# Depthwise taps as row stacks on quarters of TensorE's columns, and five PSUM banks in one pool

## The chip, the cores and the metric

The kernel runs on one core of one Trainium2 chip. The metric is the device time of one execution in microseconds. Of the kernel before, three runs gave 18203.6, 18205.7 and 18205.72 us; the median is 18205.7 us.

Names of the engines: PE is TensorE (PEld its weight loads), DVE is VectorE, ACT is ScalarE, POOL is GpSimd, and SP is the queue that issues every DMA of this kernel.

## What is computed

Two residual layers on 8 images of 56 x 56 pixels and 192 channels, all in float32. The first is a group normalisation and attention with depthwise 3x3 convolutions for queries (stride 1) and for keys and values (stride 2). The second is a state-space scan in four directions; the change touches its input, the depthwise 3x3 convolution over 384 channels, and the PSUM banks in which its scan works:

```
xz = einsum('bhwc,oc->bhwo', gn(x), in_proj_w)
xa, z = split(xz, 2)
xc = silu(depthwise_conv3x3(xa, conv_w, 'SAME') + conv_b)      # 384 channels
xs = [xc by rows, xc by columns, both reversed]                # 4 directions, 3136 steps
dts, Bs, Cs = split(x_proj_weight @ xs)                        # 12, 16 and 16 rows
delta = softplus(dt_projs @ dts + bias)
h = exp(delta * A) * h + delta * B * xs                        # 16 states a channel
y = sum over the states of h * C, + D * xs
out = x + out_proj(layernorm(y summed over the directions) * silu(z))
```

## The kernel before

**Tiling.** The 3136 pixels of an image are 7 chunks (`NCH`) of T = 448 pixels, which is 8 rows (`RPC`) of 56. The 384 channels of the second layer are NJ = 3 blocks of 128 partitions; the 192 outer channels are 2 blocks of 96.

**The scan** takes the 8 images ("batches") one after the other, each in four directions of 7 chunks with 16 states: 448 steps a batch. A step is done by these generators, each with its own line:

- `row_loads`: a DMA spreads one row of B over 128 partitions (`bb`, five buffers); for some states a row of C too (`cb`).
- `inputs_made` (L1119): POOL multiplies it with delta * x into a state tile `h` (seven buffers), 3 x 448 elements wide.
- `decays` (L1133): ACT makes three exponentials `da`, one for each channel block, each into one PSUM bank.
- `scans` (L1150): DVE runs three scans over `h` with `da`; the bank is free after its scan.
- `turned` (L1196): PE transposes `h` by quarters of 112 pixels into a PSUM bank `ht`; `scaled` (L1212): ACT copies it into `g` and multiplies with C on the way; `back` (L1230): PE transposes `g` back and adds it up in the three banks `y`. For 3 or 4 of the 16 states POOL does this instead (`by_pool`, L1248 and L1252), and `summed` (L1267) adds the result into `y`.
- `evicted` (L1282, L1284): DVE adds `y` into `yacc`.

**The front** prepares the next batch while the scan of one runs: normalisation, first-layer convolutions (L615 and L452), attention (L756, L765), then the second layer's projection `project` (L853), its depthwise convolution (L452 again), and `x_proj` (L936 to L953), which makes the rows and the steps. Batch 0's front runs alone ahead of the first scan, with eight PSUM banks to itself. `finish` (L984 to L1033) ends a batch. Batch 7 has no front beside it.

**The convolution in question.** `project` takes the channel blocks j in turn. For each chunk it makes a projection in a PSUM bank, and `xa_out` (L818) has DVE write it with its bias into `xa`, one tile of 128 x 56 x 56. Then, for each chunk, nine matmuls (`TAPS`, `conv_rows`, L452) multiply a shifted view of `xa` with a 128 x 128 diagonal matrix of one tap's weights, all adding up in one bank; at an image's border the view is cut. The diagonals come from DRAM (`dgx_d`, 576 KB a block). `xv_out` (L824) has ACT copy the bank into `xv`, one tile for a block, and `stored` applies Silu (L830) and writes both pixel orders to DRAM (`xch`, `xcw`). The next block's projections need the one `xa` free, and its convolution the one `xv`.

**What sets the order.** Every engine runs its instructions in an order that is fixed when the program is built. A small planner (`Sched`) simulates the engines: each generator yields (engine, cost, what it reads, what it writes), and the planner gives the instruction that can start first, less a rank that favours some generators. DMAs carry a landing time with a margin of 3 us. A `Ring` hands out buffers in turn; a `Share` hands out the free tile of a common set whose last use is oldest, up to a limit `most`. The front is held to a pace (`pace`): its planned PE time may run 12 us ahead of or behind a share of the batch, 87% of it over the first three directions. Where the planner sees PE idle for more than 0.45 us, it puts filler matmuls of 64 columns (`warm`, L1363).

**PSUM during the scan**: three banks for `y`; two for the exponentials, a ring (`pa`, `rda`); and three (`pb`, `three`) shared by `ht`, two at most, and by all of front and finish (`bank1`), one at most.

## Time and profile before

| | |
|---|---|
| median of three runs | 18205.7 us |
| profiled execution | 18215.8 us, of which the span of the program is 18214.1 us |
| first scan starts (end of batch 0's front and first steps) | 814 us |
| batches 0 to 7, from first scan to the next batch's | 2273, 2231, 2212, 2205, 2208, 2206, 2212, 1799 us |
| busy: PE, DVE, ACT, POOL | 16706, 14152, 14224, 15561 us |
| moved by DMA | 2159 MB, 119 GB/s; engines 39.7% busy on the main queue |
| granted PE clock, mean | 0.982 |

A line of a group reads: source line, engine, operation, output <- inputs, their shapes, count | busy time in us, mean ns of one | idle time of the engine just before them, and what released it. A line of the waits reads: who waited <- for what: us in total, times, longest. A line of the timeline reads: start, length, engine, line, operation, operands, count, and in brackets idle time before it with its releaser. Busy time of PE counts each matmul record to its modelled end, so records that follow closely overlap. A stretch's busy time counts work of all lines in it.

### The profile page before, as it was taken

To read this page: it belongs to the slowest core of one execution; us is meant where nothing else is said; L and a number is where in the kernel's file an instruction comes from. 1 tells how busy PE (TensorE), PEld (TensorE's weight loads), DVE (VectorE), ACT (ScalarE), POOL (GpSimd) and SP (SyncE) were. 2 spreads that over 40 slices of the span, in tenths; PEclk is the share of its full clock that TensorE was granted. 3 is DMA by queue.
4 is the path that set the end of the run, shared out by engine and by line. 5 is a ranking of instruction groups with operands and counts; after the bars stand their busy time and mean duration, and the time that the engine had idled before them with its cause. 6 is when DMAs were issued, how large, how long until landed. Compare 5 with 4: busy or idle time off the path is not lost. (4 is left out here: it accounts for less than half of the span.)

```text
span 18214.1 us, 279960 instructions
## 1 busy us (share of the span) xinstructions
PE 16706.4 (92%) x99872; PEld 11743.7 (64%) x99872; DVE 14151.5 (78%) x17811; ACT 14223.5 (78%) x25030; POOL 15560.9 (85%) x5200
## 2 busy tenths in 40 slices
PE   8799999999999999999999999999999999999998
PEld 4466666666666666666666666666666666667776
DVE  2277777788878788787887877878878788888998
ACT  2377788687877878778787887878888787888888
POOL 0288899888998889888898889988899888999998
PEclk9899999999999999999999999999999999999999
DMA  1353345433453334533344334553345433453332
GB/s 54 115 161 90 94 142 158 119 90 107 140 170 97 94 112 139 163 99 95 116 147 152 99 92 120 150 150 95 96 127 155 135 93 95 135 153 120 97 96 78
DMA packets 1363539, 2158.99 MB, mean 119 GB/s; under 512 B 176112, under 2 KB 1346016, under 8 KB 1359072
## 3 DMA queue, kind: packets, MB, share of 16 engines
q1 hardware_dynamic: 1362144, 2141.09, 39.7%
q8 instruction: 791, 12.96, 0.3%
q14 instruction: 604, 4.95, 0.1%
HBM read 1649.41 MB, written 491.21 MB: 118 GB/s over the span
## 5 line engine op out<-in xcount | busy, mean ns | idle before, releaser
L1150 DVE TENSOR_TENSOR_SCAN h<-da,newc,h 128x448 f32<-128x448 f32 x9216 | 10104.9, 1137 | 1970.7 <-ACT da L1133 1380.5
L1119 POOL TENSOR_TENSOR h<-du_s,bb 128x1344 f32<-128x1344 f32 x3584 | 10825.3, 3053 | 927.5 <-PE ht L1196 816.2
L1133 ACT ACTIVATE da<-dl_s,acoef 128x448 f32<-128x448 f32 x10752 | 6750.8, 638 | 1756.9 <-DVE h L1150 1705.7
L1212 ACT ACTIVATE g<-ht,ct_s 112x384 f32<-112x384 f32 x10864 | 5847.5, 575 | 936.1 <-PE ht L1196 771.3
L1230 PEld LDWEIGHTS y<-ident,g 112*128 112x128 f32 x32592 | 3564.4, 142 | 2902.0 <-ACT g L1212 1954.4
L1230 PE MATMUL y<-ident,g 112*128 112x112 f32 x32592 | 4799.3, 268 | 654.3 <-ACT g L1212 530.1
L1196 PE MATMUL ht<-ident,h 128*112 128x128 f32 x32592 | 4944.2, 276 | 122.5 <-ACT g L1212 46.6
L1196 PEld LDWEIGHTS ht<-ident,h 128*112 128x112 f32 x32592 | 3683.2, 135 | 482.7 <-DVE h L1150 147.3
L1150 DVE TENSOR_TENSOR_SCAN h<-da,h 128x448 f32<-128x448 f32 x1536 | 1607.5, 1078 | 459.6 <-ACT da L1133 410.9
L1248 POOL TENSOR_TENSOR yp<-h,cb 128x1344 f32<-128x1344 f32 x448 | 1366.3, 3050 | 407.6 <-PE y L1267 173.7
L1248 POOL TENSOR_TENSOR h<-h,cb 128x1344 f32<-128x1344 f32 x420 | 1281.6, 3051 | 292.0 <-issue 171.9
L1363 PE MATMUL y<-zeros 128*128 128x64 f32 x11648 | 1486.5, 271 | 0.0
L1363 PEld LDWEIGHTS y<-zeros 128*128 128x128 f32 x11648 | 1444.5, 194 | 50.2 <-issue 50.2
L920 POOL TENSOR_TENSOR v<-v,xs 128x1344 f32<-128x1344 f32 x224 | 677.3, 3043 | 824.7 <-DMA dl<-v 773.6
L1252 POOL TENSOR_TENSOR yp<-yp,h 128x1344 f32<-128x1344 f32 x420 | 1280.1, 3048 | 32.2
L452 PE MATMUL bank<-xa,dg 128*128 128x440 f32 (+2 forms) x3024 | 1237.1, 535 | 24.2 <-ACT xv L824 19.2
L1267 PE MATMUL y<-yp,ident 128*128 128x448 f32 x2688 | 1223.4, 546 | 10.7 <-POOL yp L1252 10.2
L756 PE MATMUL bank<-qT,kT 128*112 128x448 f32 x2352 | 1074.5, 573 | 138.6 <-DVE oT L719 82.9
L765 PE MATMUL bank<-pT,vt 112*128 112x448 f32 x2352 | 999.9, 543 | 12.4 <-ACT g L1212 6.6
L706 ACT ACTIVATE pT<-bank,nsh 112x448 f32<-112x448 f32 x1176 | 740.1, 632 | 207.2 <-PE bank L756 167.1
L452 PE MATMUL bank<-band,dgq 96*96 96x440 f32 (+3 forms) x2016 | 806.4, 532 | 10.7 <-ACT hq L582 7.7
L452 PEld LDWEIGHTS bank<-xa,dg 128*128 128x128 f32 x3024 | 525.8, 191 | 364.6 <-issue 289.9
(146 smaller groups left out, 11082.0 us busy)
## 6 DMA issues: line engine op xcount, KB each, us to landing
bb<-rows SPq DMA_DIRECT2D x3584, 224.0 KB, 3.4
cb<-rows SPq DMA_DIRECT2D x868, 224.0 KB, 3.7
dl<-v SPq DMA_DIRECT2D x224, 672.0 KB, 5.0
du<-v SPq DMA_DIRECT2D x224, 672.0 KB, 6.1
du_s<-du SPq DMA_DIRECT2D x224, 672.0 KB, 4.5
dl_s<-dl SPq DMA_DIRECT2D x224, 672.0 KB, 4.6
xt<-x1d SPq DMA_DIRECT2D x224, 336.0 KB, 4.6
xch<-xv SPq DMA_DIRECT2D x24, 1568.0 KB, 7.3
```

Source lines behind the costliest of these rows:

```text
L452: nc.tensor.matmul(out[:, o0:o1, a:b], lhs, img(lo, hi)[:, :, a + dx - 1:b + dx - 1], start=(t == TAPS[0]), stop=(t == TAPS[-1]))
L756: nc.tensor.matmul(ps.ap[:TP, :T], kts[h][:, kb * TP:(kb + 1) * TP], qh.ap, start=True, stop=True)
L1119: nc.gpsimd.tensor_tensor(h.ap, du.ap, bb.ap.unsqueeze(1).to_broadcast([128, NJ, T]), ALU.mult)
L1133: nc.scalar.activation(da.ap[:, :T], dl.ap[:, j], AF.Exp, scale=acoef[:, k * NJ + j, n:n + 1])
L1150: nc.vector.tensor_tensor_scan(h.ap[:, j, rev], da.ap[:, 0:T][:, rev], h.ap[:, j, rev], news[i - 1].ap[:, j, n:n + 1] if ci else 0.0, ALU. ...
L1196: nc.tensor.transpose(ht.ap[:TP, j * 128:(j + 1) * 128], h.ap[:, j, s * TP:(s + 1) * TP], ident)
L1212: nc.scalar.activation(g.ap, ht.ap[:TP, :DIN], AF.Copy, scale=ct.ap[:, s, n:n + 1])
L1230: nc.tensor.matmul(y["t"].ap[:, j, s * TP:(s + 1) * TP], g.ap[:, j * 128:(j + 1) * 128], ident[:TP, :TP], is_transpose=True, start=(n == 0 ...
L1248: nc.gpsimd.tensor_tensor(to.ap, h.ap, cbr.ap.unsqueeze(1).to_broadcast([128, NJ, T]), ALU.mult)
L1252: nc.gpsimd.tensor_tensor(yp.ap, yp.ap, h.ap, ALU.add)
L1267: nc.tensor.matmul(y["t"].ap[:, j, :T], ident, yp.ap[:, j], start=False, stop=(y["left"][j] == 0))
L1363: nc.tensor.matmul(ybanks[:, 0, T:T + FILL], zeros, zeros[:, :FILL], start=False, stop=False)
```

## The change

It has two parts.

**The convolution.** `xa` is no longer kept on the chip. DVE writes each projected chunk into one of two padded tiles (8 rows of 58, zeros at both ends), and a DMA stores it into a padded image in DRAM, `xpd` (58 x 58 for each channel; two of them, for even and odd batches, their outer rows set to zero once). `load_stacks` loads each chunk back three times, shifted by one row each (dy = 0, 1, 2), so that 96 partitions hold 32 channels under each of the three shifts, and the four groups of 32 channels of a block lie beside each other in the free dimension. A matmul then contracts over three vertical taps at once: `dgx_d` now holds, for each block, group and dx, a 96 x 32 matrix of three stacked diagonals. For each chunk and each dx four matmuls of 96 x 32 are issued, one for each group, into partitions 32g to 32g+31 of one bank. So 12 smaller matmuls stand for 9 full ones. The planner books the four of one dx with the cost of one, `t_mm(T)`. Projection, stack loads and convolution are three generators of their own.

**The banks.** The two banks of the exponentials and the three of `ht` and front become one set of five (`shared`), from which all three take; the limits (2, 2, 1) stay.

```diff
-    dgx_d = dconst.tile([128, NJ, 9, 128], F32, name="dgx_d")
+    dgx_d = dconst.tile([96, NJ, 4, 3, 32], F32, name="dgx_d")
+    xpd = [dconst.tile([128, NJ, HW + 2, HW + 2], F32, name=f"xpd{i}") for i in range(2)]
+    for t in xpd:
+        for row in (0, HW + 1):
+            nc.sync.dma_start(t[:, :, row], zeros[:, :HW + 2].unsqueeze(1).to_broadcast([128, NJ, HW + 2]))
...
+        id3 = taps.tile([96, 32], F32, name="id3")
+        w3 = taps.tile([96, NJ, 4, 3], F32, name="w3")
+        for dy in range(3):
+            rows = slice(32 * dy, 32 * dy + 32)
+            nc.vector.tensor_copy(id3[rows], ident[rows, rows])
+            nc.sync.dma_start(w3[rows].rearrange("c j g x -> c (j g) x"),
+                              conv_w[:, 3 * dy:3 * dy + 3].rearrange("(q c) x -> c q x", c=32))
+        for j in range(NJ):
+            d = taps.tile([96, 4, 3, 32], F32, name="d3")
+            for g in range(4):
+                for dx in range(3):
+                    nc.vector.tensor_scalar(d[:, g, dx], id3, w3[:, j, g, dx:dx + 1], None, ALU.mult)
+            nc.sync.dma_start(dgx_d[:, j], d)
...
-            def xa_out(pin, xa, j, c):
-                yield DVE, t_dve(T), pin.c + [k_nb], [xa.c[c]]
-                nc.vector.tensor_scalar(xa.ap[:, c * RPC:(c + 1) * RPC].rearrange("p h w -> p (h w)"), pin.ap[:, :T],
+            xp = xpd[b % 2]
+            padded = [fw.tile([128, RPC, HW + 2], F32, name=f"padded{i}") for i in range(2)]
+            rpad = Share([Tile(1) for _ in padded], [lambda t=t: t for t in padded], 2)
+            yield DVE, 0.8, [], []
+            for t in padded:
+                nc.vector.memset(t, 0.0)
+            k_xp = [[Cell() for _ in range(NCH)] for _ in range(NJ)]
+            stacks = {}
+
+            def xa_out(pin, j, c):
+                xa = yield rpad
+                yield DVE, t_dve(T), pin.c + [k_nb], xa.c
+                nc.vector.tensor_scalar(xa.ap[:, :, 1:HW + 1], pin.ap[:, :T].rearrange("p (h w) -> p h w", w=HW),
                                         nbias[:, j:j + 1], None, ALU.add)
                 pin.free()
+                yield from dma(xa.c, [k_xp[j][c]], 3.0, xp[:, j, 1 + c * RPC:1 + (c + 1) * RPC], xa.ap, [xa])
+
+            def load_stacks():
+                for j in range(NJ):
+                    for c in range(NCH):
+                        st = yield fi("stack", [96, 4, RPC * (HW + 2)], parts=3)
+                        for dy in range(3):
+                            src = xp[:, j, c * RPC + dy:(c + 1) * RPC + dy].rearrange("(g q) h w -> q g (h w)", q=32)
+                            yield from dma(k_xp[j][max(c - 1, 0):c + 2], [st.c[dy]], 3.0,
+                                           st.ap[32 * dy:32 * dy + 32], src)
+                        stacks[j, c] = st
...
+            def convolved():
+                for j in range(NJ):
+                    dg = yield fi("dg", [96, 4, 3, 32])
+                    yield from dma([], dg.c, 3.0, dg.ap, dgx_d[:, j])
                     xv = yield fv("xv", [128, L], parts=NCH)
                     for c in range(NCH):
+                        yield lambda: (j, c) in stacks
+                        st = stacks[j, c]
+                        stv = st.ap.rearrange("p g (h w) -> p g h w", w=HW + 2)
                         pcv = yield bank()
-                        for t in TAPS:
-                            yield PE, t_mm(T), xa.c[max(c - 1, 0):c + 2] + dg.c, pcv.c if t == 8 else []
-                            conv_rows(pcv.ap[:, :T].rearrange("p (h w) -> p h w", w=HW), dg.ap[:, t],
-                                      lambda lo, hi: xa.ap[:, lo:hi], c * RPC, RPC, t)
...
+                        for dx in range(3):
+                            yield PE, t_mm(T), st.c + dg.c, pcv.c if dx == 2 else []
+                            for g in range(4):
+                                nc.tensor.matmul(pcv.ap[32 * g:32 * g + 32, :T].rearrange("p (h w) -> p h w", w=HW),
+                                                 dg.ap[:, g, dx], stv[:, g, :, dx:dx + HW],
+                                                 start=(dx == 0), stop=(dx == 2))
+                        st.free()
                         sc.spawn(xv_out(pcv, xv, j, c))
...
-            pa = es.enter_context(tc.tile_pool(name="pa", bufs=2, space=PSUM))
-            pb = [es.enter_context(tc.tile_pool(name=f"pb{i}", bufs=1, space=PSUM)) for i in range(3)]
+            pb = [es.enter_context(tc.tile_pool(name=f"pb{i}", bufs=1, space=PSUM)) for i in range(5)]
...
-            rda = Ring(lambda: pa.tile([128, 512], F32, name="da"), 2)
-            three = [Tile(1) for _ in pb]
+            shared = [Tile(1) for _ in pb]
 
             def share(name, most):
-                return Share(three, [lambda p=p: p.tile([128, 512], F32, name=name, tag="bank") for p in pb], most)
-
+                return Share(shared, [lambda p=p: p.tile([128, 512], F32, name=name, tag="bank") for p in pb], most)
+
+            rda = share("da", 2)
             rht = share("ht", 2)
```

More of the change, by code (lines that the diff above doesn't have):

```diff
@@ L383 @@
     dgkv_d = dconst.tile([CP, NB, 9, CP], F32, name="dgkv_d")
-    dgx_d = dconst.tile([128, NJ, 9, 128], F32, name="dgx_d")
+    dgx_d = dconst.tile([96, NJ, 4, 3, 32], F32, name="dgx_d")
[3 more added lines that the diff above has]
+            nc.sync.dma_start(t[:, :, row], zeros[:, :HW + 2].unsqueeze(1).to_broadcast([128, NJ, HW + 2]))
     with tc.tile_pool(name="taps", bufs=2) as taps:
-        for dst, src, p, nb in ((dgq_d, dw_q, CP, NB), (dgkv_d, dw_kv, CP, NB), (dgx_d, conv_w, 128, NJ)):
+        for dst, src, p, nb in ((dgq_d, dw_q, CP, NB), (dgkv_d, dw_kv, CP, NB)):
             w = taps.tile([p, nb, 9], F32, name="w")
@@ L843, in project @@
                 for j in range(NJ):
-                    dg = yield fi("dg", [128, 9, 128], bufs=1)
-                    yield from dma([], dg.c, 5.0, dg.ap, dgx_d[:, j])
-                    xa = yield fv("xa", [128, HW, HW], parts=NCH)
                     for c in range(NCH):
@@ L855, in project @@
                         xt.free()
-                        sc.spawn(xa_out(pin, xa, j, c))
+                        ends.append(sc.spawn(xa_out(pin, j, c)))
+            def convolved():
+                for j in range(NJ):
+                    dg = yield fi("dg", [96, 4, 3, 32])
+                    yield from dma([], dg.c, 3.0, dg.ap, dgx_d[:, j])
                     xv = yield fv("xv", [128, L], parts=NCH)
                     for c in range(NCH):
+                        yield lambda: (j, c) in stacks
+                        st = stacks[j, c]
+                        stv = st.ap.rearrange("p g (h w) -> p g h w", w=HW + 2)
                         pcv = yield bank()
-                        for t in TAPS:
-                            yield PE, t_mm(T), xa.c[max(c - 1, 0):c + 2] + dg.c, pcv.c if t == 8 else []
-                            conv_rows(pcv.ap[:, :T].rearrange("p (h w) -> p h w", w=HW), dg.ap[:, t],
-                                      lambda lo, hi: xa.ap[:, lo:hi], c * RPC, RPC, t)
-                        if c == NCH - 1:
-                            xa.free()
-                            dg.free()
+                        for dx in range(3):
[5 more added lines that the diff above has]
+                        st.free()
                         sc.spawn(xv_out(pcv, xv, j, c))
+                    dg.free()
                     ends.append(sc.spawn(stored(xv, j)))
             lx = sc.spawn(load_x1())
-            pj = sc.spawn(project())
-            yield from sc.join([lx, pj])
+            pj = [sc.spawn(g()) for g in (project, load_stacks, convolved)]
+            yield from sc.join([lx] + pj)
             yield from sc.join(ends)
```

## The prediction

> **What bounds the kernel now.** I read the page's first part, then the busy time of each engine by stretches, then the groups and the waits of one batch, then the order of TensorE's instructions in time. The stretches below are batch 0, batch 4, batch 7 and the quiet middle of batch 7 (from the start of the first scan of a batch to that of the next). Columns: window and its length, then busy us and count for PE, weight loads, DVE, ACT and POOL, granted clock, DMA share, GB/s.
>
> ```profile
> 814.00:3087.00 2273.00, 2102.53 (x12519) 1475.68 (x12520) 1782.50 (x2246) 1787.97 (x3118) 1990.33 (x665) 0.98 0.42 127
> 9735.00:11943.00 2208.00, 2038.56 (x12139) 1426.47 (x12137) 1768.80 (x2217) 1771.05 (x3115) 1966.36 (x657) 0.99 0.42 122
> 16360.00:18159.00 1799.00, 1657.68 (x12417) 1335.23 (x12417) 1603.26 (x1946) 1567.97 (x2883) 1727.08 (x574) 1.00 0.35 101
> 16500.00:17600.00 1100.00, 1013.67 (x7928) 834.10 (x7926) 1005.50 (x1213) 963.82 (x1812) 1095.22 (x365) 1.00 0.33 97
> ```
>
> The reader is to see two regimes. In batch 7 no further batch has to be prepared, and POOL works 1095 of 1100 us: POOL is the bound, and nothing of this change touches its work. In batch 4 (and 1 to 6 alike) POOL works 1966 of 2208 us, so 242 us of it are idle; this is the most that such a batch can give. PE is busy 2039 us there, but part of it is the filler (L1363): 153 us in a middle batch and 357 us in batch 7, by the same view taken for that line. So PE has 1885 us of real work in a middle batch and 1301 in the last.
>
> The groups and the waits of batch 4 say who holds POOL:
>
> ```profile
> L1119 POOL TENSOR_TENSOR h<-du_s,bb 128x1344 f32<-128x1344 f32 x449 | 1356.6, 3053 | 129.2 <-PE ht L1196 117.5 <-DMA bb<-rows 3.1 <-PE y L1230 2.6
> L1133 ACT ACTIVATE da<-dl_s,acoef 128x448 f32<-128x448 f32 x1344 | 841.5, 638 | 221.8 <-DVE h L1150 217.5
> ...
> PEld y L1230 <- ACT g L1212: 232.9, 543, 7.5
> DVE h L1150 <- ACT da L1133: 221.7, 232, 8.6
> ACT da L1133 <- DVE h L1150: 217.5, 330, 16.2
> POOL h L1119 <- PE ht L1196: 117.5, 33, 17.1
> ```
>
> POOL waits for state buffers that PE has not yet transposed (117.5 us), PE waits for ACT's scaled copies (233 us before weight loads), and ACT is held in order before exponentials whose PSUM bank a scan still reads (217.5 us). It is a ring in which PE has the most work.
>
> The convolution itself, first in the front of batch 0, where nothing runs beside it, then in a middle batch:
>
> ```profile
> 519.02 48.19 PE L452 MATMUL bank<-xa,dg 128*128 128x448 f32 x126
> ...
> 8849.76 0.90 PE L452 MATMUL bank<-xa,dg 128*128 128x440 f32 x2
> 8850.50 0.74 PE L1230 MATMUL y<-ident,g 112*128 112x112 f32 x6
> 8851.08 0.82 PE L1196 MATMUL ht<-ident,h 128*112 128x128 f32 x6
> 8852.77 1.76 PE L452 MATMUL bank<-xa,dg 128*128 128x448 f32 x4 [0.87 <-ACT xv L824]
> ```
>
> 7 chunks x 9 taps are 63 matmuls but 126 records: each float32 matmul is two passes, one after the other, 48.19 / 126 = 0.382 us apart. A batch has 21 chunks x 18 = 378 passes, 144.6 us of PE. Beside the scan the taps stand in short runs between transposes, which use the whole array; counted over the trace, 293 runs have one tap, 239 two and 114 three, 1.72 on average.
>
> **What the Trainium skill says.** "TensorEngine Tiling (Array Packing)", Key Properties: tiles of the array work independently, and changing the tiling mode (not just the tile) drains TensorE. No run here has column tiles. "TensorE: Matmul & The Clock Gate", Measured speedup vs the span model: three column tiles gave 2.38x, and matmuls begin and end strictly in program order. The trace shows the two passes and their order, which that table (one pass each) doesn't have. "FP8 and Floating Point Precision", TensorE Precision Notes: true float32 takes four passes; the trace has two records for each matmul, so a record may hold two of them.
>
> **The change part by part.**
>
> (1) The taps. Nine 128x128 taps of a chunk become three blocks (one for each dx) of four matmuls, 96 rows by 32 columns, each on its own quarter of the columns: 63 blocks a batch, 8 passes each. Three prices for a block:
> - all quarters side by side, both passes: 2 slots of 0.382 = 0.76 us (this is also what the planner is told, 0.77);
> - in program order with two passes for each quarter: the second pass of quarter 0 needs the first to end, quarter 1's first pass can run beside it, its second comes next, and so on. A lone block takes 5 slots, a run of n takes 4n+1;
> - one after another: 8 slots = 3.06 us.
>
> Each run pays for leaving and entering the mode. A record lasts 0.54 us where its successor starts 0.375 later, so a tail is 0.165 and two are 0.33 us. With runs of 1.72 blocks: side by side (3.44 x 0.382 + 0.33) / 1.72 = 0.96 us a block, 60 us a batch; in order (7.88 x 0.382 + 0.33) / 1.72 = 1.94, 122 us; one after another 3.06 + 0.19 = 3.25, 205 us. Against 144.6: -84, -22, +60 us of PE in each of batches 1 to 7. I take the middle one, because the trace shows that passes of one matmul follow each other before the next matmul's come.
>
> What a microsecond of PE is worth: from batch 4 to batch 7 PE's real work falls by 584 us, the time by 409: 0.70 (POOL's smaller work is in it, so it may be less; where PE is the bound it is 1). So -59, -16, +42 us for each batch.
>
> (2) The detour. For every chunk DVE writes a padded copy (the same 0.67 us as L818), SP issues one store and three stack loads of some 230 KB: 84 more transfers a batch, 20 MB on 270 MB, DMA at 0.42. A transfer of this size lands after 3.2 us (xcw<-xw) to 5.0 us (qT<-qd). They stand in SP's queue among the row loads bb, behind waits; rows have five buffers, each used for one POOL step of at least 3.05 us, so a stop of some 3 us is covered four times over. Cost taken: nothing; without cover 21 x 3.2 = 67 us a batch. The 1.77 MB of taps shrink to 0.44 MB.
>
> (3) Five shared banks. Before, exponentials had two banks of their own and transposes and front three. The limits stay 2, 2, 1, so no more tiles are live in the plan, but the next exponential takes the bank that has been free longest, not the one of the scan before last. What goes is part of the 217.5 us for which ACT is held at L1133; what is late next is PE or POOL. Batch 7 gains nothing (POOL 99.6% busy). For a middle batch the gain lies between a small loss, say 10 us, where a bank is taken that PE or DVE releases later than planned, and 110 us, POOL's whole wait for ht. I take 30: about a seventh of ACT's wait; the other buffers keep the ring closed.
>
> (4) The planner. It books 0.77 us a block. If a block costs 1.94, PE falls 63 x 1.17 = 74 us behind its written order in the convolution's stretch. The order alone costs nothing so long as the other engines have work queued; at worst 0.70 x 74 = 52 us a batch. Taken: nothing.
>
> (5) The front of batch 0, exposed. Today 219 us pass from the first projection (495) to the last tap (714): 3 x 48 us of taps, the rest projections that wait for the one xa buffer and for x1 loads. After: projections run ahead under the taps. Middle price: 21 x (13 x 0.382 + 0.33 [one mode change a chunk]) = 111 us, some 34 us while the single xv buffer is copied out twice (567 to about 584 today), 18 us for the first store and load: about 162, so -57. Side by side the two stack buffers limit it, about 4.5 us a chunk: 95 + 52 = 147, -72. One after another: 21 x 9.3 + 52 = 247, +28. Setup before (27 tap products and three stores against 39 small ones, seven small loads and three stores) is equal within a few us.
>
> **The sum**, against the profiled execution's 18215.8 us (span 18214.1; 10 us above the median of 18205.7): seven batches x (-16 - 30) = -322, front -57: -379, so 17837 us. I give 17840.
>
> **The rivals.**
> - All quarters side by side: 7 x (-59 - 30) - 72 = -695, 17520 us. For it: tiles are said to be independent. Against: order of passes as above.
> - Slower: quarters one after another. Place: the 63 blocks of a batch. 7 x (+42 - 30) + 28 = +112, 18330 us; with nothing from the banks 18540. It decides from the point where a block takes more than 2.3 us (144.6 / 63), less what the banks give. For it: no float32 column tile is in any trace here, and streaming four moving operands may not be possible at four bytes. Against: the skill's packing table.
> - SP holds the rows: stack loads wait in the queue for their stores, and the 67 us of (2) come uncovered: 7 x 67 = +469 on the sum, 18310 us. Against: POOL's wait for bb is 3 us in a whole batch now.
> - The parts cancel: the 52 us of (4) come in full and eat the gain, 17840 + 364, about 18200.
>
> **Chances and range.** In order 0.40, side by side 0.22, one after another 0.24, SP 0.08, cancelled 0.06. A measurement of this kernel tells about 0.2% from no change. Faster 0.62, within 0.2% 0.06, slower 0.32. The likeliest case alone, with banks from 0 to 80 us, spans 17490 to 18050; with most of the first two rivals 17430 to 18430.
>
> **What would show it.** The chunk's matmuls of 96x32 should be 24 records; in the front of batch 0 a chunk takes about 5.3 us of PE if passes go in order, 2.6 if side by side, 9.3 if one after another. ACT's wait at L1133 for scans should fall from 217 us in a middle batch and POOL's for ht from 117; batch 7 should stay at 1799. The prediction is wrong if POOL waits for bb, if a middle batch loses less than 20 us, or if the conv's stretch has POOL idle for longer than now.

## The result, and the profile after

The changed kernel takes 17889.8 us (median of four runs, 17887.5 to 17908.3) against 18205.7 us before: a ratio of 0.983, with a 95% interval from 0.981 to 0.985. The forecast was 17840 us; the time lies inside its range. That the total came out so near is luck: two steps of the sum were far off, in opposite directions, as the sections below show.

The profiled execution spans 17885.7 us, 328 us less than before. Where they went, from the first scan of a batch to the first scan of the next, and for batch 7 to the start of its last scan (worked out from the starts of the scans in both traces; `finish` after it takes 55 us before and 57 after):

| stretch | before | after | difference | forecast |
|---|---|---|---|---|
| to the first scan | 813.9 | 745.2 | -69 | -57 |
| batch 0 | 2272.9 | 2278.4 | +5 | -46 |
| batches 1 to 6, mean | 2212.2 | 2173.7 | -38.5 each, -231 in all | -46 each |
| batch 7 | 1799.2 | 1763.5 | -36 | 0 |

The view of busy time by stretches for the kernel after, for the same four stretches as before (batch 0, batch 4, batch 7, the quiet middle of batch 7; columns as there):

```profile
745.00:3024.00 2279.00, 2067.68 (x12579) 1431.90 (x12580) 1786.80 (x2260) 1796.65 (x3123) 2001.75 (x670) 0.97 0.46 138
9553.00:11722.00 2169.00, 1976.73 (x12195) 1379.56 (x12195) 1767.78 (x2219) 1770.46 (x3115) 1965.16 (x657) 0.98 0.45 133
16066.00:17829.00 1763.00, 1593.71 (x11730) 1261.95 (x11729) 1576.91 (x1935) 1566.68 (x2876) 1719.24 (x572) 1.00 0.34 101
16250.00:17350.00 1100.00, 991.57 (x7572) 800.51 (x7572) 997.03 (x1223) 980.10 (x1830) 1098.51 (x366) 1.00 0.32 97
```

PE's real work in batch 4 (less the filler, 156 us by the view of that line) is now 1821 us instead of 1885. POOL's work is the same 1965 us and its idle time fell from 242 to 204. PE lost 64 us, the batch only 39. That PE lost no more has a reason that the profile shows: counting each record from its start to the start of the next one, the convolution holds PE for 90 us less in this batch, but the transposes of `h` and `g` hold it for 975 us instead of 945.

The groups and the waits of batch 4, after (the lines of the code have moved by 46: L1165 is the old L1119, L1179 the old L1133, L1242 the old L1196, L1258 the old L1212):

```profile
L1165 POOL TENSOR_TENSOR h<-du_s,bb 128x1344 f32<-128x1344 f32 x449 | 1355.4, 3051 | 77.2 <-PE ht L1242 58.3 <-DVE qe L610 10.6 <-DMA bb<-rows 5.2
L1179 ACT ACTIVATE da<-dl_s,acoef 128x448 f32<-128x448 f32 x1344 | 821.6, 635 | 86.3 <-DVE h L1196 43.4 <-DVE nsh L701 11.7 <-DVE padded L847 6.9
```

```profile
PEld y L1276 <- ACT g L1258: 190.1, 516, 3.4
ACT g L1258 <- PE ht L1242: 188.9, 250, 7.2
DVE h L1196 <- ACT da L1179: 176.0, 180, 9.3
...
POOL h L1165 <- PE ht L1242: 58.3, 17, 12.3
```

The same wait of ACT for `ht` in the kernel before:

```profile
ACT g L1212 <- PE ht L1196: 106.9, 149, 4.9
```

ACT's wait for a scan's bank fell from 217 to 43 us and POOL's wait for PE's transposes from 117 to 58. But ACT now waits 189 us for `ht`, where it waited 107 before: a part of the wait has moved from one of ACT's instructions to another. Rows (`bb`) are late for 5 us in the batch, so SP does not starve POOL.

The order of TensorE's instructions in time, first in the front of batch 0, then beside the scan:

```profile
511.83 4.71 PE L908 MATMUL bank<-stack,dg 96*32 96x448 f32 x24 [0.86 <-DMA stack<-xpd]
...
578.68 2.46 PE L908 MATMUL bank<-stack,dg 96*32 96x448 f32 x24
582.23 2.46 PE L908 MATMUL bank<-stack,dg 96*32 96x448 f32 x24 [1.08 <-DMA stack<-xpd]
```

```profile
11002.82 2.46 PE L908 MATMUL bank<-stack,dg 96*32 96x448 f32 x24
11005.21 0.79 PE L1276 MATMUL y<-ident,g 112*128 112x112 f32 x6
11005.84 0.82 PE L1242 MATMUL ht<-ident,h 128*112 128x128 f32 x6
```

A chunk's 12 matmuls are 24 records, and they take 2.46 us in all. That is the forecast's "2.6 if side by side", not its "5.3 if in order". The starts of the 24 records, in us from the first, read from single records of the chunk at 578.68:

```
pass 1 of dx 0: 0.000 0.007 0.013 0.020     pass 2: 0.375 0.407 0.414 0.421
pass 1 of dx 1: 0.750 0.783 0.790 0.797     pass 2: 1.125 1.159 1.166 1.172
pass 1 of dx 2: 1.501 1.535 1.542 1.548     pass 2: 1.877 1.911 1.917 1.924
```

The four quarters start within 20 to 50 ns of each other, and each quarter's second pass follows its own first pass. Counted from start to start, the convolution holds PE for 53 us in a batch (142 before), and for 66 us in the front of batch 0 (143 before).

The issues of the new transfers:

```profile
stack<-xpd SPq DMA_DIRECT2D x504, 232.0 KB, 4.7
xpd<-padded SPq DMA_DIRECT2D x168, 232.0 KB, 4.7
```

A chunk's way through DRAM is thus about 4.7 + 4.7 us of landing, at the upper end of the 3.2 to 5.0 us that were assumed.

### The profile page after: what moved, and what is told of

It reads as the page before. It is cut to its first block, busy times and chain, and to the rows that moved or that the text cites. A ratio compares the mean times of both kernels' runs of the same rounds, so it can differ in the third digit from the quotient of the medians.

```text
span 17885.7 us, 277600 instructions
## 1 busy us (share of the span) xinstructions
PE 16160.6 (90%) x99800; PEld 11302.8 (63%) x99800; DVE 14114.4 (79%) x17839; ACT 14223.1 (80%) x25030; POOL 15550.4 (87%) x5200
## 5 line engine op out<-in xcount | busy, mean ns | idle before, releaser
L1196 DVE TENSOR_TENSOR_SCAN h<-da,newc,h 128x448 f32<-128x448 f32 x9216 | 10077.2, 1136 | 1781.7 <-ACT da L1179 1184.3
L1165 POOL TENSOR_TENSOR h<-du_s,bb 128x1344 f32<-128x1344 f32 x3584 | 10818.6, 3052 | 613.8 <-PE ht L1242 502.2
L1258 ACT ACTIVATE g<-ht,ct_s 112x384 f32<-112x384 f32 x10864 | 5928.9, 577 | 1596.5 <-PE ht L1242 1386.1
L1179 ACT ACTIVATE da<-dl_s,acoef 128x448 f32<-128x448 f32 x10752 | 6582.2, 636 | 741.1 <-DVE h L1196 391.6
L1276 PE MATMUL y<-ident,g 112*128 112x112 f32 x32592 | 4865.3, 268 | 649.4 <-ACT g L1258 458.7
L1242 PE MATMUL ht<-ident,h 128*112 128x128 f32 x32592 | 5181.5, 277 | 221.5 <-DVE h L1196 136.2
L1242 PEld LDWEIGHTS ht<-ident,h 128*112 128x112 f32 x32592 | 3679.2, 135 | 847.1 <-DVE h L1196 392.8
L1196 DVE TENSOR_TENSOR_SCAN h<-da,h 128x448 f32<-128x448 f32 x1536 | 1590.9, 1076 | 394.7 <-ACT da L1179 258.6
L1408 PE MATMUL y<-zeros 128*128 128x64 f32 x10568 | 1423.6, 274 | 0.0
L1408 PEld LDWEIGHTS y<-zeros 128*128 128x128 f32 x10568 | 1377.1, 198 | 49.0 <-issue 49.0
L775 PEld LDWEIGHTS bank<-qT,kT 128*112 128x112 f32 x2352 | 365.3, 178 | 537.0 <-issue 142.3
L999 PE MATMUL bank<-xd,dtw 128*128 128x448 f32 x1344 | 626.5, 572 | 33.3 <-DVE sz L1060 8.8
```

The lines of the kernel that those rows point to most:

```text
L775: nc.tensor.matmul(ps.ap[:TP, :T], kts[h][:, kb * TP:(kb + 1) * TP], qh.ap, start=True, stop=True)
L1165: nc.gpsimd.tensor_tensor(h.ap, du.ap, bb.ap.unsqueeze(1).to_broadcast([128, NJ, T]), ALU.mult)
L1179: nc.scalar.activation(da.ap[:, :T], dl.ap[:, j], AF.Exp, scale=acoef[:, k * NJ + j, n:n + 1])
L1196: nc.vector.tensor_tensor_scan(h.ap[:, j, rev], da.ap[:, 0:T][:, rev], h.ap[:, j, rev], news[i - 1].ap[:, j, n:n + 1] if ci else 0.0, ALU. ...
L1242: nc.tensor.transpose(ht.ap[:TP, j * 128:(j + 1) * 128], h.ap[:, j, s * TP:(s + 1) * TP], ident)
L1258: nc.scalar.activation(g.ap, ht.ap[:TP, :DIN], AF.Copy, scale=ct.ap[:, s, n:n + 1])
```

## The experiments

Twelve kernels were run, each for a question. All their times, in us; the first four columns are read from the trace of one execution (batch 7 to the start of its last scan), the ratio is to the kernel before on the same chip (18203.6 to 18212.1 us there). Both kernels with three taps leave out six of the nine taps:

| kernel | first scan | batch 0 | batches 1-6, mean | batch 7 | median | ratio, 95% interval |
|---|---|---|---|---|---|---|
| before | 813.9 | 2272.9 | 2212.2 | 1799.2 | 18205.7 | |
| after | 745.2 | 2278.4 | 2173.7 | 1763.5 | 17889.8 | 0.983 (0.981-0.985) |
| banks alone | 807.9 | 2285.0 | 2219.4 | 1778.3 | 18258.1 | 1.002 (1.0015-1.003) |
| convolution alone | 743.9 | 2271.2 | 2197.6 | 1789.1 | 18045.4 | 0.991 (0.989-0.992) |
| quarter by quarter | 765.7 | 2296.7 | 2200.4 | 1764.1 | 18103.8 | 0.994 (0.992-0.995) |
| pace with ACT | 747.9 | 2314.7 | 2217.4 | 1737.8 | 18156.7 | 0.997 (0.996-0.998) |
| copies on DVE | 741.9 | 2294.4 | 2214.6 | 1763.3 | 18114.3 | 0.9955 (0.994-0.997) |
| three taps, old banks | 716.6 | 2243.4 | 2154.4 | 1780.2 | 17726.7 | 0.974 (0.972-0.975) |
| three taps, shared banks | 714.1 | 2239.8 | 2144.5 | 1763.9 | 17641.1 | 0.969 (0.968-0.9705) |
| slower pace | 741.3 | 2262.3 | 2170.0 | 1774.7 | 17837.6 | 0.980 (0.978-0.981) |
| lead of four | 763.2 | 2271.7 | 2173.5 | 1754.4 | 17893.5 | 0.983 (0.9815-0.984) |
| loads twice | 929.5 | 2463.7 | 2366.8 | 1763.7 | 19418.4 | 1.067 (1.065-1.069) |
| lead and slower pace | 764.9 | 2274.4 | 2143.3 | 1776.9 | 17730.7 | 0.974 (0.973-0.9755) |
| the same, not in batch 0 | 746.7 | 2273.7 | 2143.5 | 1775.9 | 17720.6 | 0.973 (0.972-0.975) |

### Which part brings it: each alone

Banks alone, in the kernel before:

```diff
-            pa = es.enter_context(tc.tile_pool(name="pa", bufs=2, space=PSUM))
-            pb = [... for i in range(3)]
+            pb = [... for i in range(5)]
-            rda = Ring(lambda: pa.tile([128, 512], F32, name="da"), 2)
-            three = [Tile(1) for _ in pb]
+            shared = [Tile(1) for _ in pb]
...
+            rda = share("da", 2)
```

> The kernel before with nothing changed but the five shared banks. Theory A (both parts gain): ACT's wait for scans at the exponentials falls from 217 us in a middle batch to under 150, and the time is 100 to 210 us under before, 18000 to 18110 us. Rival B (the banks give nothing, the whole gain is the convolution's): within 40 us of before, 18165 to 18245. Rival C (the banks give most): under 17960. Batch 7: A and C expect some 1760 us, since nothing else can have shortened it; B 1799.

Measured: 18258 us, 0.2% slower than before and outside all three forecasts. The waits of batch 4 of this kernel:

```profile
ACT g L1212 <- PE ht L1196: 235.6, 291, 7.6
...
POOL h L1119 <- PE ht L1196: 120.3, 31, 18.0
...
ACT da L1133 <- DVE h L1150: 45.8, 93, 4.9
```

ACT's wait for a scan's bank falls as in the full change (217 to 46 us). But ACT then waits 236 us for `ht` (107 before), and POOL still waits 120 us for it. PE has no less to do than before (from start to start its transposes hold it for 966 us of batch 4, before for 945), so the wait changes its name and is not gained. Why the transposes take longer with shared banks is not shown.

The convolution alone is the changed kernel with the two sets of banks put back, which is the diff above read backwards.

> The changed kernel with the banks of before (two for the exponentials, three for the rest), so the convolution alone. The front of batch 0 must keep its 69 us (no scan runs there). Theory A: the rest gains little because the stretch of the convolution gives back what other stretches gain, 18040 to 18110 us. Rival B: 17870 to 17930, all of the gain. Rival C: 18130 or more, only the 69 us.

Measured: 18045 us, as theory A expected for this part. The parts do not add: -167 and +46 us alone (the kernel before took 18212 beside them), -316 together. With the new convolution in place the banks take off 24 us in each of batches 1 to 6; on the kernel before they add 7.

### The price of a block: quarter by quarter

The two inner loops change places, so that a quarter's three matmuls follow each other in program order. The planner's cost for a chunk is the same.

```diff
-                        for dx in range(3):
-                            yield PE, t_mm(T), st.c + dg.c, pcv.c if dx == 2 else []
-                            for g in range(4):
+                        for g in range(4):
+                            yield PE, 0.75 * t_mm(T), st.c + dg.c, pcv.c if g == 3 else []
+                            for dx in range(3):
```

> The changed kernel with the loops over quarter and dx exchanged: the three matmuls of one quarter stand together in the program, then those of the next quarter. If each quarter runs its own line of matmuls regardless of the program's order, a chunk in the front of batch 0 still takes about 2.5 us and the time stays within 40 us of 17890. If a matmul can't start before the one ahead of it in the program has started, a quarter's second matmul waits for its first and holds all behind it: nine steps of 0.75 us, 6.8 us a chunk, some 90 us of PE more in a batch, and about 18200 to 18350 us.

The timeline of PE in the front of batch 0 of this kernel:

```profile
532.49 7.92 PE L908 MATMUL bank<-stack,dg 96*32 96x448 f32 x48
540.34 3.27 PE L890 MATMUL bank<-xt,wx 96*128 96x448 f32 x8
```

Two chunks take 7.92 us, 3.96 each instead of 2.46. From the single records, each quarter's six passes still follow each other at 0.375 us, and the next quarter's first pass comes 0.78 us after this one's first, not after its last (2.26 us). So the next quarter is held up for two passes and not for six: its first pass starts when the third matmul of this quarter, which stands ahead of it in program order, cannot have started (it would need four passes before it, 1.5 us). This is neither the strict order nor the free running between which the expectation chose. PE's occupation by the convolution rises from 53 to 86 us in a batch, and batches 1 to 6 take 26.7 us longer: 0.81 us of time for each us of PE.

### Is ACT the bound beside the convolution? Two misses

In the kernel after, the scan's chunks beside projection and convolution (chunks 17 to 21 of batch 4, counted from 0) take 87.8, 79.8, 90.6, 82.2 and 90.2 us. In the kernel before the same chunks take 75.5, 69.0, 70.5, 72.6 and 86.1, although its convolution stands in chunks 15 to 20. Chunks 2 to 16 are 5.1 us shorter on the mean (single ones from 19 us longer to 21 shorter). So the change loses something in this stretch, and the first theory (called D in the expectations) was ACT: the convolution now passes in 156 us instead of 387, with ACT's `xv` and `xw` copies in this shorter time.

If so, a pace that counts ACT's planned work too should spread the stretch:

```diff
-        if s.group is not None and e == PE:
+        if s.group is not None and e in (PE, ACT):
```

> The changed kernel, but the pace of the front counts planned time of PE and ACT together instead of PE alone. Theory D (the convolution's stretch, now 190 instead of 400 us long, carries the same 51 us of ACT work of its own, so ACT at 93% busy bounds it): the stretch grows to over 230 us, its chunks fall from some 84 to 78 us or less, and the time falls to 17650 to 17800 us. Rival E (what holds that stretch is the landing of stacks or the single front bank): the chunks stay as long, and the time stays within 50 us of 17890 or grows.

Measured: 18157 us, 267 more than the kernel after; the convolution still passes in about 155 us. The edit changed the pace of everything else and not what it was meant to change, so it does not test the theory.

Then the copies were moved to DVE:

```diff
-                yield ACT, t_act(T), pcv.c, [xv.c[c]]
-                nc.scalar.activation(xv.ap[:, c * T:(c + 1) * T], pcv.ap[:, :T], AF.Identity, bias=cb[:, j])
+                yield DVE, t_dve(T), pcv.c, [xv.c[c]]
+                nc.vector.tensor_scalar(xv.ap[:, c * T:(c + 1) * T], pcv.ap[:, :T], cb[:, j], None, ALU.add)
...
-                    yield ACT, t_act(T), [k1], xw.c
-                    nc.scalar.copy(xw.ap, xv.ap.rearrange("p (h w) -> p w h", w=HW)[:, c * RPC:(c + 1) * RPC])
+                    yield DVE, t_dve(T), [k1], xw.c
+                    nc.vector.tensor_copy(xw.ap, xv.ap.rearrange("p (h w) -> p w h", w=HW)[:, c * RPC:(c + 1) * RPC])
```

> The changed kernel with the evictions xv and the seven transposing copies xw of each block moved from ACT to DVE, 35 us of ACT work a batch. Theory D (ACT, 93% busy in the convolution's stretch, bounds it): that stretch gets 15 us or more shorter in each of seven batches, 17720 to 17800 us. Rival E (the chain of store, stack loads and matmuls, with PE serving it ahead of the scan, sets the stretch): no gain, 17880 us or more, since DVE's scans now stand behind the copies.

Measured: 18114 us, and the five chunks of the stretch take 89 to 101 us, longer than with the copies on ACT. Taking work off ACT does not help; as DVE, which runs the scans, got the copies, this run alone does not say that ACT is no bound. But in the kernel after ACT is busy for 258 of the 340 us of the stretch, 76% (the fourth engine in the line of this stretch further down), and for 86% of the busiest 190 us in it, not for the 93% of the expectation. Theory D is not borne out.

### What the detour costs: PE relieved without it

To take the detour through DRAM out of the comparison, the kernel before ran with three of its nine taps, (4, 5, 8); the other six are left out of the computation. That is 126 records a batch, 48 us of PE by 0.382 us each, close to the 53 us of the new convolution. `xa` stays on the chip.

```diff
-                        for t in TAPS:
+                        for t in (4, 5, 8):
```

> The kernel before with three of the nine taps of this convolution (the centre, right of it, and below right); six are left out, so PE has as little to do as with quarters side by side, without the detour through DRAM and with the old banks. If the detour is free, this is the time of the convolution alone (e2, 18045 us) within 40 us. If the detour costs in the convolution's stretch, it is under that by 15 us or more for each of seven batches, 17880 to 17960 us.

And the same with the shared banks (the diff of the banks added; the same six taps left out):

> As the run with three of nine taps, but with the five shared banks. Theory F (the banks pay only where PE has slack, because ACT, freed of the wait for scans, runs into the wait for PE's transposes): with PE relieved as here the banks take off 100 to 200 us, as they do between e2 and the changed kernel (160), although alone they cost 46. Rival G (the gain of the banks in the changed kernel comes from the order that happened to be planned around stacks): with taps the banks again give less than 50 us. If the detour costs, this run is also under the changed kernel's 17890 by about 100 us.

Measured: 17727 and 17641 us. Both are far faster than their counterparts with the whole convolution (18045 with old banks, 17890 with shared ones), and the first is faster than either of its forecasts; the banks take off 86 us here, where theory F expected 100 to 200 and G under 50. Read by batches 1 to 6:

- PE's relief of 94 us (142 to 48) is worth 58 us with old banks (2212.2 to 2154.4) and 75 with shared ones (2219.4 to 2144.5): 0.61 and 0.80 us for each us of PE.
- The detour costs 43 us with old banks (2154.4 to 2197.6) and 29 with shared ones (2144.5 to 2173.7), of which 3 to 4 us are the 5 us more of PE. Ahead of the first scan it costs 27 and 31 us, in batch 0 28 and 39.
- The banks take off 10 us here, between the +7 of the kernel before and the -24 of the new convolution, and 86 us over the whole run.

So the lighter PE by itself turns the banks from a loss into a gain, and beside the detour they are worth more still. Why more is not shown. In batch 4 of the two kernels with shared banks all of the detour's cost lies in one place: chunks 17 to 21 take 401 us with three taps and 431 with the detour, chunks 0 to 16 take 1269 and 1268, the rest 471 and 470. But the same five chunks took 374 us in the kernel before, so 27 us of what this stretch lost are there without the detour.

### How the detour costs: pace, lead and SP's queue

Three things were suspected: the stretch is too short for what it moves; the projection runs up to a block ahead of the convolution, so that transfers crowd and PE is booked onto stacks that have not landed (J in the expectations); and the chain of store and loads through SP's in-order queue is long (K).

A slower pace: each block of the convolution counts twice in the planned PE time that holds the front back.

```diff
                         for dx in range(3):
                             yield PE, t_mm(T), st.c + dg.c, pcv.c if dx == 2 else []
+                            sc.spent["front"] += t_mm(T)
```

> The changed kernel, but each block of the convolution counts twice its planned PE time in the pace of the front, so that the front is pressed less in that stretch. Theory H (front work pressed together there gives back what the thinner front elsewhere gains): the stretch grows from some 157 us to 190 or more, its chunks fall under 80, and the time falls to 17750 to 17850. Rival: PE work only moves to other stretches, which get longer by as much, 17860 to 17930 us.

Measured: 17838 us, 52 less than the kernel after. The convolution passes in 226 us instead of 156 in batch 4; batch 3 falls to 2142 us, but batches 1 and 2 take 2221 and 2184.

A lead of at most four chunks, counted by `turned_`, which `convolved` raises after each chunk:

```diff
+            turned_ = [0]
...
-                        yield lambda: (j, c) in tiles
+                        yield lambda: (j, c) in tiles and j * NCH + c < turned_[0] + 4
...
+                        turned_[0] += 1
```

> The changed kernel, but a projection may be at most four chunks ahead of the last chunk convolved, so that projections, matmuls on stacks, evictions and copies of one block lie beside each other. Theory J (the detour costs 30 us a batch in the convolution's stretch because nothing holds the projections back any more, as the one xa did: first 21 projections press on PE and DVE, then all evictions and copies on ACT): the stretch's chunks fall towards those of three taps, 15 to 30 us less in each of seven batches, 17680 to 17790 us. Rival K (it is the length of the chain of store, loads and matmuls, or SP's queue): no gain or a loss, 17880 us or more, since less is prepared ahead.

Measured: 17893 us, no difference from the kernel after, as rival K expected. The crowding of the projections alone is not the cause.

Every stack load issued twice, the second waiting in SP's queue for the first to land; the planner books nothing for it:

```diff
-                            yield from dma(k_xp[j][max(c - 1, 0):c + 2], [st.c[dy]], 3.0,
-                                           st.ap[32 * dy:32 * dy + 32], src)
+                            yield SP, 0.07, k_xp[j][max(c - 1, 0):c + 2], [st.c[dy]], 3.0
+                            for _ in range(2):
+                                nc.sync.dma_start(st.ap[32 * dy:32 * dy + 32], src)
```

> The changed kernel with every stack load issued twice, in the same planned order: 63 more loads and 15 MB more in a batch, and the second waits for the first, so a stack takes twice as long to come and SP's queue is held the longer. Rival K expects a large loss, another 30 us or more for each of seven batches, over 18100 us. Theory J expects less than 10 us for each, under 17970 us, most of it in the front of batch 0.

Measured: 19418 us; batches 1 to 6 take 193 us longer each than in the kernel after. The stretch of the convolution in batch 4 of this kernel, first by busy time and then by SP's own waits ("SPq" is SP's queue):

```profile
11820.00:12268.00 448.00, 270.76 (x1635) 160.48 (x1634) 196.46 (x240) 201.31 (x345) 211.14 (x70) 0.77 0.54 151
```

```profile
SPq L860 <- DMA stack<-xpd: 223.2, 63, 8.0
...
SPq L485 <- POOL h L1166: 6.9, 5, 3.3
```

and two of the engines' waits:

```profile
PE bank L909 <- DMA stack<-xpd: 109.5, 15, 9.8
...
POOL h L1166 <- DMA bb<-rows: 51.7, 6, 20.5
```

SP stands 223 us for its 63 pairs of loads, 3.5 us each, and the batch loses 193, nearly as much. POOL is busy for 211 of 448 us. Two ways in which this reaches the end are seen, and this run does not separate them: the stacks come late to PE, which waits 110 us for them, and rows come late to POOL, which waits 52. The stretch beside the convolution in the kernel before, by busy time and by the same view of SP's waits:

```profile
11035.00:11435.00 400.00, 370.83 (x2194) 261.05 (x2193) 315.85 (x386) 329.52 (x571) 367.48 (x123) 0.99 0.43 127
```

```profile
SPq L466 <- POOL h L1119: 179.7, 57, 9.3
```

and of the kernel after (340 us of projection, convolution and what stands between):

```profile
SPq L485 <- ACT xw L876: 43.2, 16, 5.9
SPq L485 <- PE bank L890: 35.7, 10, 15.8
SPq L485 <- POOL h L1165: 32.3, 15, 4.9
```

When SP waits for POOL's `h`, a row load is at the head of its queue and only lacks a free buffer: SP is ahead of the scan. Before, that was 180 of 400 us; after, 32 of 340; with loads twice, 7 of 448. This is the cover that the forecast relied on, and the change uses most of it up. The view does not show that SP sets the end in the kernel after: rows were late for only 5 us there. It shows how little was left. In the kernel with lead and slower pace, which comes next, it is 68 of 368 us.

Now both together, lead of four and slower pace; the diff is that of the two kernels above.

> Projections at most four chunks ahead, and the blocks of the convolution counted twice in the pace. If the two remedies add up (52 us by the pace alone): 17650 to 17750 us, under every complete version so far. If they work on the same loss: within 30 us of the better of the two.

Measured: 17731 us. Batches 1 to 6 take 2143.3 us, 30 less than in the kernel after, and as little as with three taps, shared banks and no detour (2144.5). So these batches cost no more than three taps do at the old pace, with every one of the detour's 84 transfers still in place. That the detour itself costs nothing any more is not shown: three taps were not run at the slower pace, which may have a gain of its own. In batch 4 chunks 17 to 21 take 369 us here against 401 with three taps, and the chunks before them 1301 against 1269. The view of one tile's instructions, here `stack` from 1000 to 17600 us; after "idle before" each line gives microseconds and times. Kernel after:

```profile
its engine sat idle before it (us, times) until:
  issue: 199.2, 651
  DMA stack<-xpd: 71.3, 41
...
who waited for it (us, times):
  ACT xv L864: 169.5, 128
```

Lead and slower pace:

```profile
  issue: 130.1, 466
...
  DMA stack<-xpd: 15.8, 11
...
  ACT xv L865: 67.6, 42
```

PE sits idle for stacks that have not landed for 16 us instead of 71, and ACT waits 68 us for the convolution's banks instead of 170. Landing takes no less (5.1 us in the median, 4.7 in the kernel after); the stacks are asked for earlier before PE's turn. From single records of the later batches, in the median: a stack's last load has landed 13.1 us before its first matmul, against 1.5 us in the kernel after, 3.0 with the lead alone and 4.5 with the pace alone. With the lead alone PE still waits 67 us, with the pace alone 38. Busy time in the stretch of projection and convolution in batch 4, first of the kernel after, then of this one (POOL is the fifth engine):

```profile
10822.00:11162.00 340.00, 290.32 (x2084) 200.17 (x2083) 254.96 (x304) 258.41 (x442) 272.72 (x91) 0.94 0.68 187
```

```profile
10650.00:11018.00 368.00, 331.80 (x2379) 220.17 (x2376) 309.13 (x377) 300.20 (x536) 339.25 (x113) 0.98 0.65 178
```

POOL works 92% of the stretch instead of 80%: 113 of its instructions in 368 us, where the kernel after would need 422 us at its 91 in 340. This is where the batches gain: chunks 17 to 21 take 62 us less than in the kernel after, the chunks ahead of them some 32 more. The direct waits of PE explain 55 of the 186 us that batches 0 to 6 gained together; the rest lies in what stands behind PE and ACT and was not taken apart.

The lead also holds the projection back ahead of the first scan, which comes 20 us later. So the limit was lifted for the front of batch 0:

```diff
-                        yield lambda: (j, c) in tiles and j * NCH + c < turned_[0] + 4
+                        yield lambda: (j, c) in tiles and (b == 0 or j * NCH + c < turned_[0] + 4)
```

> The changed kernel with the convolution's planned time counted twice in the front's pace and the projection held to 4 chunks ahead of the convolution, as in the run before that had both, but the limit of 4 holds for batches 1 to 7 only: in the front of batch 0 the projection runs as far ahead as it likes. The front of batch 0 has no scan beside it that stacks could come late for; the limit there only makes PE wait for the chain projection, store, stack loads. If so, the first scan starts at about 745 us as in the changed kernel instead of 765, the later batches stay at about 2140 us, and the time is about 17710 us, 20 less than with the limit everywhere (17731). If the limit in batch 0 is not what made the first scan late there, it stays at 765 and the time at 17730.

Measured: the first scan comes at 746.7 us again, the later batches stay, and the time is 17721 us, the best of the kernels that compute everything: 169 us (0.9%) under the changed kernel and 485 (2.7%) under the one before. It still lies 80 us above three taps with shared banks (71 by the spans of the profiled executions): 33 ahead of the first scan, where no scan runs beside the landings, 34 in batch 0, 12 in batch 7 and 6 less in the others. Those in batches 0 and 7 stay unexplained.

## Why the prediction was right, and where its steps were wrong

The forecast of 17840 us was 50 us too low. Its steps, in its own order:

**(1) The taps: mis-sized.** The term was 1.94 us a block ("in program order"), 22 us less of PE and 16 us less time in a batch. Measured is 0.84 us a block (53 us by 63), 89 us less of PE. The "side by side" price of 0.96 was the right one, and even a little too high, since the six blocks of two chunks mostly stay together (60 of 88 runs beside the scan have 48 records) where runs of 1.72 were assumed. (The 1.72 also leaves out seven runs of 29 taps and one of 7; with them the mean is 2.0 and the middle price 1.88, which changes little.) The reason given for the middle price, that passes of one matmul follow each other before the next matmul's come, was read from matmuls on the whole array and does not carry over to quarters. "TensorEngine Tiling (Array Packing)", Key Properties, says that tiles work independently, and this trace agrees where the quarters take turns, but not where a quarter's matmuls stand together. The strict order of "TensorE: Matmul & The Clock Gate" (it stands there under The mechanism), as it was read in the forecast, would have every second pass hold up the next quarter's first; with four quarters in turn it does not, and quarter by quarter a quarter holds up the next for 0.78 us, less than strict order would. Each us of PE was priced at 0.70; the runs gave 0.61 to 0.81. So this step alone was worth 54 to 72 us a batch, not 16. The price is per us of the convolution alone; all of PE's real work fell by 64 us, since its transposes took longer.

**(2) The detour: the step that failed.** Taken as nothing, with 67 us as its uncovered price. It costs 29 us in each of batches 1 to 6, 39 in batch 0 and 31 ahead of the first scan in the kernel as changed. The argument looked at whether rows would be late, and they are not (5 us a batch). What came late were the stacks at PE's in-order queue, with the scan's transposes behind them. The forecast did not ask who waits for the new transfers themselves. PE's direct waits for stacks are 10 us a batch of it (71 over seven); the rest lies in what stands behind PE and was not taken apart. Of the forecast's three signs of being wrong, two stayed away. The third, POOL idle for longer in the convolution's stretch, depends on the measure: from first to last tap in batch 4 POOL is idle for 36 of 387 us before and 34 of 155 after, and in chunks 17 to 21 for 32 us before and 81 after.

These two errors cancel, by luck. Added up in one order, for each of batches 1 to 6: the lighter PE takes off 58 us (old banks), the detour adds 43, the banks take off 24, together 39. The forecast had 16, nothing and 30, together 46.

**(3) The banks: right in size where it was put, wrong in reason.** Taken as 30 us; measured 24 in batches 1 to 6, in the company of the new convolution. The forecast read the gain from ACT's 217 us alone. That wait went in banks alone as well (to 46 us), and the kernel became slower. What turns it into a gain is PE with time to spare, which the forecast did not make a condition, though its range allowed for a small loss. Batch 7 was said to gain nothing because POOL is 99.6% busy. It gained 36 us: 18 in its first chunk (119.6 to 101.2 us), the rest in chunks of 60.2 instead of about 60.9 us, with POOL at 99.9%. Banks alone gave 21 of it and the convolution alone 10: the first chunk is shorter with the convolution alone (105.6), the later ones with the banks alone (60.2).

**(4) The planner.** The block costs 0.84 where the planner is told 0.77, so the case that was priced did not arise, and taking nothing for it was right. But the planner does have a hand in it: its order puts the convolution's matmuls where stacks have not landed, as the runs with pace and lead show (1.5 us from landing to matmul, and 13.1).

**(5) The front of batch 0.** Forecast -57, measured -69, near the -72 of the side-by-side case. From the first tap to the last 134 us pass, where 195 passed before. The way through DRAM adds to it: three taps without the detour start the first scan 31 us earlier still.

**Batch 0** was counted like the other batches at -46 and came out at +5. Its relief is there (three taps, old banks: -30), but detour and banks took it back.

**The rivals.** Side by side was right about the price of a block and wrong about the total, since it left the detour at nothing as well. SP holding the rows did not happen (5 us), but the run with loads twice shows that it begins not far off (52 us in the stretch). Quarters one after another did not happen, in either order of the loops. The parts did cancel in a way, but not by a PE that falls behind its written order: a good part of PE's gain went into the detour (29 of 75 us with shared banks, 43 of 58 with the old ones).

## What to carry to other kernels

Price a detour through DRAM by who waits for its last landing, not only by whether the queue has room: here the engine that consumes it stood in an in-order queue with the critical work behind it. Here two things together made its transfers of 5 us come in time, a producer held close ahead of its consumer and a consumer pressed less: 159 us together, where the pace alone gave 52 and the lead alone nothing. A freed buffer pays only if the engine that comes next has time: measure such a part on its own and in company before it is credited.

## What was not expected of the hardware

- Four float32 matmuls of 96 x 32 on four quarters of the columns, each with two passes, start within 50 ns of each other, and the four take what one of 128 x 128 takes: 24 records in 2.46 us, six slots of 0.375 us and a tail.
- Going between quarters and the whole array is cheap. In the kernel with lead and slower pace, at the full clock, a run of one, two or three blocks takes 0.89, 1.64 and 2.39 us from its start to the start of the next instruction, which is 0.75 a block and 0.14 a run. After a transpose `ht` a block starts 0.20 us behind it, where a tap on the whole array started 0.11 us behind it in the kernel before. So a run pays some 0.23 us for both ways. In that kernel 230 of 308 runs hold a single block, and the convolution still holds PE for only 54 us a batch.
- If a quarter's matmuls are written one after another, a quarter holds the next one back for two passes (0.78 us), not for six.
- The same 24 records took 4.71 us at 511.8 us and 2.46 us at 531.7 us. "TensorE: Matmul & The Clock Gate", Part 1, says that the clock is halved after an idle stretch, which agrees: PE was idle for 7.5 of the 8.2 us from 484.0 to 492.1, and the granted clock was 0.50 from 487 to 521 us, 0.67 on the mean from 505 to 530 and 1.00 from 530 to 545. It came back only at 521, although PE was busy for 27 of the 29 us before. With loads twice, where PE waits for stacks, the median of these matmuls over the batches was 954 ns instead of 538 and the granted clock 0.77 in the stretch; from start to start the convolution held PE for 85 us of batch 4 instead of 52. So a wait for a transfer there costs by itself and by the slower clock beside it.
